# A fused attention and ternary feed-forward kernel: ternary weights from magnitude and sign, six heads of the first pair turned by another route, and one step of the tail put elsewhere

## The chip, the cores and the metric

The kernel runs on one core of a Trainium2 chip. A core has five engines with a queue of instructions each: TensorE (PE in the profile; its weight loads are PEld), VectorE (DVE), ScalarE (ACT), GpSimd (POOL) and SyncE (SP, which only issues transfers). The engines share the on-chip memory SBUF; TensorE writes its results to the accumulators in PSUM. Each engine works through its queue in order and waits at an instruction until what it needs is there. The metric is the device time of one execution in microseconds. Before the change it is 1085.36 us, the median of 3 runs (1084.41 to 1085.46).

## The reference

Sixteen sequences of 256 tokens with 256 features go through an attention layer and a feed-forward layer, each between two layer norms and added to its input. Cut to what is computed:

```python
# attention; H = 16 heads of D = 128
q = (x @ Wq.T).reshape(b, n, H, D)
kp, vp = split(x @ Wkv.T)                 # one K and one V for all heads
kh, vh = cumsum((x @ Wkvh.T) * exp(cumsum(log_sigmoid(x @ Wg.T))))   # one number per head and token
k, v = kp * kh, vp * vh                   # so the heads differ by a factor per token
p = softmax(causal(rope(q) @ rope(k).T / sqrt(D)))
attention = (p @ v).reshape(b, n, H * D) @ Wout.T

# feed-forward; hidden size 1024
def ternary_quant(w):                     # groups of 64 weights
    w = w.astype(bfloat16)
    scale = max(mean(abs(w_group)), 1e-8)
    q = clip(round(w / scale), -1, 1)     # -1, 0 or 1
    return w + (q * scale - w)
gate, up = split(x @ ternary_quant(w_gate_up).T)
ffn = rms_norm(silu(gate) * up) @ ternary_quant(w_proj).T

x = x + layernorm(attention(layernorm(x)))
x = x + layernorm(ffn(layernorm(x)))
```

## The kernel before

**Tiling.** Two sequences make a pair, so that a pair has 512 columns (T); there are 8 pairs. Pair and head together number 128 *slots*: slot g deals with pair g // 16 and head g % 16, in a software pipeline. `slot(g)` writes out, for all engines, the scores of head g; the division of the probabilities of head g-1 by their row sums and the turning of that 256x256 matrix (the product with the values needs it transposed); the keys of head g+2 (`keys`, L659, on POOL); the query product of head g+1 (g+2 in the first four slots) and its rotation on DVE (L347, L355, L358); and the outputs of an earlier head, which ACT copies to `oT` (L802). The projection of the heads and the feed-forward of the pair finished before run in the same slots as guests.

**Order.** Nothing is scheduled at run time. The order in which the program writes instructions is the order of each engine's queue. Guests are put into named places of a slot (first, scored, turned, emptied, projection, last) with `put(slot, place, step, key)`, and the table `MOVED` (L13 to L38) shifts a step by its key through these places, by so many places earlier or later. After slot 127 the function `end()` writes the tail out by hand: the feed-forward of the last three sequences, named there c, a and b (b is sequence 15).

**Two ways to turn probabilities.** `Head.on_pe` (L601) chooses. True: `turn_on_pe` has TensorE transpose three 128x128 blocks for each sequence of the pair (L757) into PSUM, and ACT copies them to SBUF in two pieces each (L762), multiplying by the head's value factors on the way; the outputs then use the shared values, and are written in the same slot. False: ACT's division (L723) writes its four results into the tile `even` in an order by 32 columns; `turn` has DVE transpose all 32x32 blocks at once (L730), SP writes the tile to a buffer in the chip's memory (`moved`, L737) and reads it back with the blocks in their places in four transfers (`pT`, L743); `scale_values` has POOL make this head's values (`vph`, L771), and the outputs (L787, L794) are written one slot later. Before the change, `on_pe` is true for the 16 heads of pair 0 and for the last two heads of the last pair; the other 110 heads go by DVE.

**Ternary weights.** The feed-forward weights come as 12 blocks of 128x512 (8 of gate and up, `gu`, and 4 of the projection, `p`), each handled by one object of `Ternary`. Block i starts around slot 1 + 3i/2, so that the 12 blocks stretch over slots 0 to about 21, shifted by `MOVED` (keys T0 to T11). The steps of one block:

- `load` (L194): POOL issues the transfer of the block in float32.
- `magnitudes` (L198): ACT takes the absolute value, as bfloat16 (`ab`).
- `narrow` (L208): POOL casts the weights to bfloat16 (`wb`). Two tiles t0 and t1, of two halves each, hold `wb`, `sc`, `up` and `dn`.
- `sums` (L212): TensorE multiplies `ab` by a block matrix of ones, so that each row gets the sum of its group (`wsum`).
- `compare`: DVE makes the scale `sc` (L216), then `up` = (edge · sc < wb) at L219 and `dn` = (-edge · sc > wb) at L222. `up - dn` is the ternary digit.
- `combine` (L228 to L231): POOL takes up - dn, times sc, minus wb, plus wb.
- `write` (L234): ACT copies the result to the weights that TensorE reads.

**Tail.** The end of `end()` turns the last projections into output rows. For sequence b: `project(2)`, then `project_rows(0)` and `project_rows(1)`, each the last matmuls (L981) of 128 rows into one half of the accumulator `ffn`; `end_moments(t)` (L1064, L1065: moments of one half, DVE), `end_factors`, `end_centred` and `end_rows(t)` (the row update on DVE and the store by SP). They are interleaved with those of sequence a.

Of the kernel before, what the change touches and what calls it, by code (L numbers as in the profile page):

```python
# [37 lines left out]
AF = mybir.ActivationFunctionType  # L38
ALU = mybir.AluOpType
# [4 lines left out]
H, D = 16, 128  # L44
# [17 lines left out]
TERNARY_EDGE = 257.0 / 512.0  # L62
# [3 lines left out]
def sandwich_kernel(  # L66
# [13 lines left out]
    nc = tc.nc  # L80
# [15 lines left out]
    pairs = B // BP  # L96
# [28 lines left out]
    def load_wq(first, end):  # L125
        cols = slice(first * D, end * D)
        nc.sync.dma_start(
            out=wq_sb[:, :, cols], in_=wq[:, cols].rearrange("(c p) f -> p c f", p=P)
        )
# [55 lines left out]
    def hidden_tile(shape, dtype, name):  # L185
        return p1.tile(shape, dtype, tag="h", name=name, bufs=5)

    class Ternary:
        def __init__(self, dst, src, name):
            self.dst, self.src, self.name = dst, src, name  # L190
# [7 lines left out]
            nc.scalar.activation(self.ab, self.w, AF.Abs)  # L198

        def narrow(self):  # L200
            self.wb, self.sc, self.up, self.dn = (
                pair[:, k, :]
                for pair in [
                    hidden_tile([P, 2, T], BF16, f"t{j}_{self.name}") for j in range(2)
                ]
                for k in range(2)
            )
            nc.gpsimd.tensor_copy(self.wb, self.w)  # L208

        def sums(self):  # L210
            self.total = mm_tile([P, T], f"wsum_{self.name}")
            nc.tensor.matmul(self.total, blocks, self.ab, start=True, stop=True)  # L212

        def compare(self):
            sc, wb = self.sc, self.wb
            nc.vector.tensor_scalar(  # L216
                sc, self.total, 1.0 / GROUP, 1e-8, ALU.mult, ALU.max
            )
            nc.vector.scalar_tensor_tensor(  # L219
                self.up, sc, TERNARY_EDGE, wb, ALU.mult, ALU.is_lt  # L220
            )
            nc.vector.scalar_tensor_tensor(  # L222
                self.dn, sc, -TERNARY_EDGE, wb, ALU.mult, ALU.is_gt
            )

        def combine(self):
            up = self.up
            nc.gpsimd.tensor_sub(up, up, self.dn)  # L228
            nc.gpsimd.tensor_mul(up, up, self.sc)
            nc.gpsimd.tensor_sub(up, up, self.wb)  # L230
            nc.gpsimd.tensor_add(up, up, self.wb)  # L231
# [140 lines left out]
    class Pair:  # L372
# [195 lines left out]
        def plan(self):  # L568

            end = self.bp * H  # L570
            pre = "P." if self.bp > 1 else "Q."
            s = end - H - (2 if self.bp > 1 else -1)
            for b in range(BP):
                put(s + b, "scored", lambda b=b: self.moments(b), key=f"{pre}mom{b}")
                put(s + b, "emptied", lambda b=b: self.normalise(b), key=f"{pre}nor{b}")
                put(s + 2 + b, "turned", lambda b=b: self.transpose(b), key=f"{pre}tp{b}")
                put(s + 2 + b, "emptied", lambda b=b: self.keep(b), key=f"{pre}keep{b}")
            put(s + 4, "last", self.factors, key=f"{pre}hg")
            put(s + 5, "first", self.gates, key=f"{pre}gate")
            put(s + 5, "scored", self.raw_factors, key=f"{pre}raw")  # L580
            put(s + 5, "last", self.keys, key=f"{pre}kp")
            put(s + 7, "scored", lambda: self.rope.sine(0), lambda: self.rope.sine(1), key=f"{pre}ksin")
            put(s + 7, "emptied", self.keys_done, key=f"{pre}kr")
            chain = end - (7 if self.bp > 1 else 8)
            put(chain - 2, "emptied", self.sigmoids, key=f"{pre}sig")
            put(chain - 1, "emptied", self.decays, key=f"{pre}dec")
            put(chain, "scored", self.decayed, key=f"{pre}decd")
            put(chain + 1, "scored", self.sums, key=f"{pre}sum")
            put(chain + 2, "first", self.rows_out, key=f"{pre}rows")
            put(chain + 3, "last", self.value_factors, key=f"{pre}vh")  # L590
            put(chain + 4, "first", self.value_factors_done, key=f"{pre}vhd")
            put(end - 1, "last", self.values, key=f"{pre}val")
            put(end, "first", self.values_done)


    class Head:
        def __init__(self, pair, h):
            self.pair, self.h = pair, h
            self.tag = f"{pair.bp}_{h}"

            self.on_pe = pair.bp == 0 or pair.bp == pairs - 1 and h >= H - 2  # L601

        def fetch_on_pe(self):

# [668 lines left out]
    def end():  # L1273

        c, a, b = afters[B - 3 :]
# [133 lines left out]
        a.end_centred(1)  # L1409
        b.project(2)  # L1410
        b.project_rows(0)
        b.end_moments(0)
        a.end_rows(0)
        b.end_factors(0)
        b.project_rows(1)
        a.end_rows(1)
        b.end_moments(1)
        b.end_factors(1)
# [49 lines left out]
    for g in range(total):  # L1468
        slot(g)
    end()  # L1470


# [37 lines left out]
```

## Time and profile before

| what | value |
|---|---|
| median of 3 runs | 1085.36 us |
| profiled execution | 1085.46 us, its span 1083.7 us |
| PE busy | 1067.4 us (98%) |
| DVE busy | 846.4 us (78%) |
| ACT busy | 734.5 us (68%) |
| POOL busy | 670.7 us (62%) |
| mean bandwidth of the transfers | 127 GB/s |
| comparisons L219 and L222 | 12 each |
| groups of three transposes L757 | 32 in pair 0, 4 in the last pair |
| start of slots 11, 14, 17, 18, 21 on PE | 97.34, 119.10, 140.87, 147.09, 169.92 us |

The page describes one execution. "Busy" is the time in which an engine has an instruction running; the matmul times are modelled, and as matmuls overlap, a row's mean is longer than the pace at which they follow each other. Where a row ends with "[1.10 <-PE ffn L981]", the engine stood idle for 1.10 us before it, and PE's instruction of line 981 is what it waited for. In a row of the costliest groups, the first two numbers are the busy sum in us and the mean of one in ns; behind the next bar stand the idle time before such instructions and what ended most of it. In a table of stretches the columns are the stretch, its length, and the busy time of PE, PEld, DVE, ACT and POOL with the number of instructions in brackets, then the mean granted clock of TensorE, the busy share of the transfer engines and their GB/s. A slot's start is taken as the start of its first score product (L671) on PE.

### The profile page before, as it was taken

To read this page: it belongs to the slowest core of one execution; us is meant where nothing else is said; L and a number is where in the kernel's file an instruction comes from. 1 tells how busy PE (TensorE), PEld (TensorE's weight loads), DVE (VectorE), ACT (ScalarE), POOL (GpSimd) and SP (SyncE) were. 2 spreads that over 40 slices of the span, in tenths; PEclk is the share of its full clock that TensorE was granted. 3 is DMA by queue.
4 is the path that set the end of the run, shared out by engine and by line. 5 is a ranking of instruction groups with operands and counts; after the bars stand their busy time and mean duration, and the time that the engine had idled before them with its cause. 6 is when DMAs were issued, how large, how long until landed. Compare 5 with 4: busy or idle time off the path is not lost.

```text
span 1083.7 us, 18439 instructions
## 1 busy us (share of the span) xinstructions
PE 1067.4 (98%) x5704; PEld 854.3 (79%) x5704; DVE 846.4 (78%) x2306; ACT 734.5 (68%) x2151; POOL 670.7 (62%) x705
## 2 busy tenths in 40 slices
PE   8999999999999999999999999999999999999997
PEld 5767767788788877888778887888868888788897
DVE  6888989877887779868798777978789677876565
ACT  4877866666776658576586766766577675867663
POOL 5966897338555676457665576655756546736443
PEclk9999999999999999999999999999999999999998
DMA  6312134454444444444354444445444444443200
GB/s 229 112 53 77 62 112 153 148 169 122 141 141 134 146 132 141 146 133 143 126 148 134 144 145 132 146 122 160 131 130 151 125 135 136 152 138 111 69 11 30
DMA packets 108625, 137.34 MB, mean 127 GB/s; under 512 B 12208, under 2 KB 76208, under 8 KB 108528
## 3 DMA queue, kind: packets, MB, share of 16 engines
q1 hardware_dynamic: 105696, 129.02, 38.7%
q0 software_dynamic: 2000, 6.56, 1.8%
q8 instruction: 46, 0.75, 0.3%
q10 hardware_dynamic: 832, 0.59, 0.2%
q14 instruction: 51, 0.42, 0.1%
HBM read 88.41 MB, written 47.71 MB: 126 GB/s over the span
## 4 chain that ended last, share of the span: by engine, by line
PE 89%; DVE 8%; ACT 1%; issue 1%; POOL 0%; DMA 0%; DVEq 0%; POOLq 0%; ACTq 0%
PE qps L325 19%; PE att L831 18%; PE sps L671 14%; PE ops L787 9%; PE ffn L981 6%; PE ups L885 5%; PE gps L885 5%; PE ops L794 5%; DVE turned_q L347 2%; PE hg L325 1%; PE vps L325 1%; DVE prob L684 1%; PE kp L325 1%; DVE qps L355 1%; DVE qT L358 1%; PE tps L757 1%
## 5 line engine op out<-in xcount | busy, mean ns | idle before, releaser
L684 DVE CUSTOM_DVE_ANT_0 prob<-sps,mask 128x128 f32<-128x128 f32 (+1 forms) x512 | 160.9, 354 | 122.4 <-PE sps L671 119.3
L802 ACT COPY oT<-ops 128x512 f32<-128x512 f32 x128 | 75.0, 586 | 257.5 <-PE ops L794 257.4
L325 PE MATMUL qps<-xnT,wq_sb 128*128 128x512 f32 x512 | 241.8, 594 | 0.8
L694 ACT ACTIVATE prob<-prob,low 128x128 f32<-128x128 f32 (+1 forms) x512 | 225.7, 444 | 18.3 <-DVE low L684 18.1
L831 PE MATMUL att<-wout_sb,oT 128*128 128x256 f32 x1024 | 237.7, 379 | 0.0
L831 PEld LDWEIGHTS att<-wout_sb,oT 128*128 128x128 f32 x1024 | 188.5, 190 | 30.2 <-issue 8.6
L771 POOL TENSOR_TENSOR vph<-vp,vh 128x512 f32<-128x512 f32 x110 | 115.9, 1054 | 132.1 <-PE ops L794 132.0
L671 PE MATMUL sps<-kT,qT 128*128 128x128 f32 (+1 forms) x1024 | 192.1, 331 | 4.1 <-DVE qT L358 2.2
L347 DVE TENSOR_TENSOR turned_q<-qps,sin_sb 64x512 f32<-64x512 f32 (+1 forms) x258 | 176.0, 682 | 15.0 <-PE qps L325 9.5
L659 POOL TENSOR_TENSOR kT<-kh,kr 128x512 f32<-128x512 f32 x128 | 164.6, 1286 | 7.9 <-PE sps L671 7.2
L723 ACT ACTIVATE even<-prob,total 128x128 f32<-128x128 f32 (+1 forms) x440 | 163.9, 447 | 1.1 <-DVE total L705 1.1
L671 PEld LDWEIGHTS sps<-kT,qT 128*128 128x128 f32 x1024 | 145.0, 191 | 21.4 <-issue 7.3
L325 PEld LDWEIGHTS qps<-xnT,wq_sb 128*128 128x128 f32 x512 | 95.2, 190 | 71.7 <-issue 61.6
L787 PE MATMUL ops<-pT,vph 128*128 128x256 f32 x440 | 131.3, 380 | 0.9 <-POOL lo L931 0.7
L931 POOL TENSOR_TENSOR lo<-h,hi 128x512 fp32r<-128x512 f32 x54 | 69.1, 1279 | 97.3 <-ACT hi L929 93.1
L730 DVE STREAM_TRANSPOSE sq<-even 128x768 f32<-128x768 f32 x110 | 107.5, 977 | 13.9 <-ACT even L723 10.9
L694 ACT ACTIVATION_READ_ACCUMULATOR prob<-prob,low 128x1 f32 x512 | 96.9, 189 | 0.0
L355 DVE TENSOR_TENSOR qps<-qps,cos_sb 128x512 f32<-128x512 f32 (+1 forms) x129 | 89.5, 694 | 4.6
L794 PEld LDWEIGHTS ops<-pT,vph 128*128 128x128 f32 x440 | 83.5, 190 | 11.4
L358 DVE TENSOR_TENSOR qT<-qps,turned_q 128x512 f32<-128x512 f32 (+1 forms) x129 | 88.5, 686 | 4.5
L949 POOL TENSOR_TENSOR squares<-squares,sq 128x512 f32<-128x512 f32 x39 | 49.8, 1277 | 63.3 <-ACT sq L948 63.3
L794 PE MATMUL ops<-pT,vph 128*128 128x128 f32 x440 | 84.5, 274 | 0.0
(167 smaller groups left out, 1924.8 us busy)
## 6 DMA issues: line engine op xcount, KB each, us to landing
moved<-sq SPq DMA_DIRECT2D x110, 384.0 KB, 2.3
pT<-moved SPq DMA_DIRECT2D x440, 96.0 KB, 2.2
kh<-rows SPq DMA_DIRECT2D x126, 256.0 KB, 3.4
xt<-in_x_dram SPq DMA_DIRECT2D x15, 256.0 KB, 3.0
out_dram<-y POOLq DMA_DIRECT2D x13, 256.0 KB, 3.3
wout_sb<-in_wout_dram SPq DMA_DIRECT2D x2, 1024.0 KB, 9.6
w_gu<-in_wgu_dram POOLq DMA_DIRECT2D x8, 256.0 KB, 3.4
wq_sb<-in_wq_dram SPq DMA_DIRECT2D x1, 1536.0 KB, 9.5
```

Source lines behind the costliest of these rows:

```text
L325: nc.tensor.matmul(ps, lhs[:, c, :], rhs[:, c, :], start=(c == 0), stop=(c == EC - 1))
L347: self.engine.tensor_mul(by_sequence(self.turned[a : a + HALF, :]), by_sequence(self.src[b : b + HALF, :]), over_sequences(sin_sb[b : b + ...
L659: nc.gpsimd.tensor_mul(self.kT, self.kh, self.pair.kr)
L671: nc.tensor.matmul(sps[:, cols], self.qT[:, n0 + i * P : n0 + (i + 1) * P], self.kT[:, n0 : n0 + (i + 1) * P], start=True, stop=True,)
L684: nc.vector.tensor_tensor_reduce(out=prob[:, cols], in0=sps[:, cols], in1=mask[:, P - i * P :], scale=-SCALE, scalar=F32_MAX, op0=ALU.add, ...
L694: nc.scalar.activation(prob[:, cols], prob[:, cols], AF.Exp, bias=low[:, i : i + 1], scale=-1.0, accum_out=self.total[:, b * 2 + i : b * 2 ...
L723: nc.scalar.activation(dst, src, AF.Copy, scale=self.total[:, 2 * b + i : 2 * b + i + 1])
L771: nc.gpsimd.tensor_mul(self.vp, self.pair.vp, self.pair.vh[:, :, self.h : self.h + 1].to_broadcast([P, NT, D]),)
L787: nc.tensor.matmul(ops[:, n0 : n0 + N], self.vp[:, b * (N // P), :], early, start=True, stop=False,)
L794: nc.tensor.matmul(ops[:, n0 + P : n0 + N], self.vp[:, b * (N // P) + 1, :], late, start=False, stop=True,)
L831: nc.tensor.matmul(self.acc[:, t, :], oT[:, n0 + t * P : n0 + (t + 1) * P], wout_sb[:, h, :], start=(h == 0 and t == 0), stop=(h == H - 1) ...
L885: nc.tensor.matmul(ps[:, k, :], wgu_sb[:, c, (f0 + k) * P : (f0 + k + 1) * P], part[:, c, :], start=(i == 0), stop=(i == len(steps) - 1),)
```

## The change

Three things change.

1. *Ternary.* `narrow` gets a second step: ACT writes the sign of the weights (-1, 0 or 1) where `dn` was. `compare` makes one comparison instead of two, of the scale with the magnitude `ab`. `combine` begins with `up * sign` instead of `up - dn`. Everything else of a block, and the places of its steps, stay.
2. *Heads.* `on_pe` is true only for heads 0 to 9 of pair 0. Heads 10 to 15 of pair 0, which are turned in slots 11 to 16, take the way over DVE, SP's transfers and POOL, and their outputs are written one slot later: slot 11 then has no outputs, and slots 12 to 17 have those of heads 10 to 15. (In the kernel before, slot 17 is the one without: head 0 of pair 1 is written in slot 18.)
3. *Tail.* `b.project_rows(1)` stands directly behind `b.project_rows(0)`, ahead of the moments of the first half, instead of behind `b.end_factors(0)`.

```diff
 def narrow(self):
-    self.wb, self.sc, self.up, self.dn = (
+    self.wb, self.sc, self.up, self.sign = (
...
     nc.gpsimd.tensor_copy(self.wb, self.w)
+    nc.scalar.activation(self.sign, self.w, AF.Sign)
...
 def compare(self):
-    sc, wb = self.sc, self.wb
+    sc = self.sc
     nc.vector.tensor_scalar(
         sc, self.total, 1.0 / GROUP, 1e-8, ALU.mult, ALU.max
     )
     nc.vector.scalar_tensor_tensor(
-        self.up, sc, TERNARY_EDGE, wb, ALU.mult, ALU.is_lt
-    )
-    nc.vector.scalar_tensor_tensor(
-        self.dn, sc, -TERNARY_EDGE, wb, ALU.mult, ALU.is_gt
+        self.up, sc, TERNARY_EDGE, self.ab, ALU.mult, ALU.is_lt
     )
...
 def combine(self):
     up = self.up
-    nc.gpsimd.tensor_sub(up, up, self.dn)
+    nc.gpsimd.tensor_mul(up, up, self.sign)
     nc.gpsimd.tensor_mul(up, up, self.sc)
     nc.gpsimd.tensor_sub(up, up, self.wb)
     nc.gpsimd.tensor_add(up, up, self.wb)
...
 class Head:
-    self.on_pe = pair.bp == 0 or pair.bp == pairs - 1 and h >= H - 2
+    self.on_pe = pair.bp == 0 and h < 10 or pair.bp == pairs - 1 and h >= H - 2
...
 def end():
     b.project_rows(0)
+    b.project_rows(1)
     b.end_moments(0)
     a.end_rows(0)
     b.end_factors(0)
-    b.project_rows(1)
     a.end_rows(1)
     b.end_moments(1)
```

The places in which `slot(g)` writes what belongs to the two ways:

```python
if before and not before.on_pe:
    before.turn()                  # DVE transpose, SP's five transfers
if before and before.on_pe:
    before.turn_on_pe(0)           # PE, ACT
if g + 2 < total:
    all_heads[g + 2].keys()        # POOL
all_heads[g + ahead].queries()     # PE
if before and not before.on_pe:
    before.scale_values()          # POOL
if before and before.on_pe:
    before.turn_on_pe(1)
...
if before and before.on_pe:
    before.outputs()
if 2 <= g < total + 2 and not all_heads[g - 2].on_pe:
    all_heads[g - 2].outputs()
```

## The prediction

> **What bounds the kernel now.** I read the page's head and chain first, then the stretch in which the edited heads and weight blocks lie, then the last 10 us.
>
> ```profile
> span 1083.7 us, 18439 instructions
> PE 1067.4 (98%) x5704; PEld 854.3 (79%) x5704; DVE 846.4 (78%) x2306; ACT 734.5 (68%) x2151; POOL 670.7 (62%) x705
> PE 89%; DVE 8%; ACT 1%; issue 1%; POOL 0%; DMA 0%; DVEq 0%; POOLq 0%; ACTq 0%
> 97.34:169.92 72.58, 69.91 (x331) 50.41 (x330) 63.83 (x169) 55.38 (x176) 63.22 (x63) 1.00 0.30 97
> ```
>
> TensorE is the bound, and the clock is full. The last line (busy PE, PEld, DVE, ACT, POOL from the start of slot 11 to that of slot 21) shows something the page's averages hide: here POOL is busy for 63.2 of 72.6 us, DVE for 63.8, PE for 69.9. Work moved from PE to DVE and POOL goes to engines with 9 us of slack each.
>
> **Part 1: six heads turned elsewhere.** The page gives a transpose 273 ns, but matmuls are pipelined; what counts is when the next group starts:
>
> ```profile
> 120.50 0.49 PE L757 MATMUL tps<-ident,prob 128*128 128x128 f32 x3
> 120.83 1.88 PE L325 MATMUL qps<-xnT,wq_sb 128*128 128x512 f32 x4
> L730 DVE STREAM_TRANSPOSE sq<-even 128x768 f32<-128x768 f32 x110 | 107.5, 977 | 13.9 <-ACT even L723 10.9
> L771 POOL TENSOR_TENSOR vph<-vp,vh 128x512 f32<-128x512 f32 x110 | 115.9, 1054 | 132.1 <-PE ops L794 132.0
> ```
>
> Three transposes hold PE for 120.83-120.50 = 0.33 us, so 6 heads x 2 groups x 0.33 = **3.9 us** leave PE (by the busy row it would be 9.8). ACT loses four PSUM copies per head (L762, 1.21 us from the start of the first to that of what follows, 7.3 in all); its four divisions stay at 446 ns, writing another layout. Added: 6 x 0.98 = 5.9 us on DVE, 6 x 1.01 (start to start) = 6.1 us on POOL, and per head five DMAs on SP: one of 384 KB, four of 96 KB. These sit behind the key fetch of the same slot and ahead of the next; that fetch feeds a product two slots later. From the end of a DVE transpose (144.06) to the last of its four issues (148.33) plus 2.2 us to land is 6.4 us; outputs now stand one slot later, about 7.7 us after the transpose, so some 1.3 us remain. The loads of x for pair 2 queue behind these too; the second would go out near 124.7 instead of 114.8 and is wanted at 128.
>
> Could DVE take it? In slots 11 to 16 it loses four of part 2's comparisons (0.68, 2.09, 2.07, 0.68 = 5.5 us) and gains 5.9. Per slot it then has scores 1.41, transpose 0.95, rotation of the next queries 1.42 + 0.73 + 0.61, reciprocal 0.1: 5.2 us; a weight block adds 0.66 + 0.69, the moments of pair 2 0.95. PE has scores 1.4, queries 1.72, projection 1.73, outputs 1.3: 6.15, in slot 11 no outputs, which come back in slot 17. The rotation ends after PE in slots 11 (103.4 against 102.5) to 16, so DVE releases the next scores. Adding these rows with small gaps, slots 12 to 17 start at 103.4, 110.2, 117.0, 124.1, 131.8, 138.4; before at 104.7, 111.6, 119.1, 126.2, 134.0, 140.9. The lead is **2.5 us** at slot 17.
>
> **Part 2: magnitude and sign.** Twelve L222 comparisons leave DVE, 13.7 us busy; twelve Sign calls join ACT, not in the trace. Lower bound 0 (hidden), upper the sibling Abs on the same tile, 632 ns; I take its pace, 0.53. The multiplication by the sign costs POOL what the subtraction did (1.16).
>
> ```profile
> 112.89 2.09 DVE L222 SCALAR_TENSOR_TENSOR t_gu<-t_gu 128x512 bf16<-128x512 bf16 x1
> 113.14 1.28 POOL L659 TENSOR_TENSOR kT<-kh,kr 128x512 f32<-128x512 f32 x1
> L694 ACT ACT_TABLE_LOAD x13 | 16.7, 1283 | 0.2
> ```
>
> Two rules bear on this. The Trainium skill, *ScalarE: Activation LUTs*, "Table sets: the hidden batching unit", says that functions come in sets that must be loaded, and names relu, copy, identity and abs as those that every set has. Sign is not named there. If it were missing from Exp's set, every block would cost two loads, 24 x 1.283 = 30.8 us of ACT; the trace shows Abs between Exps without a load and cannot show Sign. I take none, and keep 30.8 as a remote end. *SBUF — State Buffer*, "Who interferes with whom", says a DVE instruction with two SBUF inputs and a GpSimd one exclude each other, the later waiting out the earlier. The rows differ with overlap: L222 took 2.09 us beside the key product, 0.68 elsewhere. By the rows part 2 frees 13.7 us; by the rule it frees 12 x 0.68 = 8.2 of work, and the six added POOL products bring back new collisions for the twelve comparisons that stay (up to 2.3 each, if one meets a key product and a value product). DVE has 2.5 us to spare before slot 17, so I count nothing for this, and 1 us in the range.
>
> In slots 2 to 4 ACT holds PE (chain from 29.92 to 33.65). Two Signs come before the divisions of head 2: 2 x 0.53, less 0.3 of wait that is there, puts PE 0.75 us back; it regains it at 47.95, where it waited 0.7 us behind a comparison. Slots 5 to 10 have 0.7 us of PE idle in all. Net 0 (-0.5 to +0.3).
>
> **Where the lead of 2.5 us goes.** Five lines around slot 17, whose last PE item is the sum over block 10 (wsum_p):
>
> ```profile
> 103.68 0.78 POOL L194 DMA_DIRECT2D w_p<-in_wproj_dram  x1 [3.37 <-ACT ab_gu L198]
> 143.18 1.16 POOL L231 TENSOR_TENSOR t_p<-t_p,t_p 128x512 bf16<-128x512 bf16 x1
> 144.70 1.13 ACT L234 CAST wproj_sb<-t_p 128x512 fp32r<-128x512 bf16 x2
> 145.72 0.63 ACT L198 ACTIVATE ab_p<-w_p 128x512 bf16<-128x512 f32 x1
> 146.41 0.38 PE L212 MATMUL wsum_p<-ab_p,blocks 128*128 128x512 bf16 x1 [0.18 <-ACT ab_p L198]
> ```
>
> POOL ends block 9 at 144.3, ACT copies it, takes block 10's magnitudes, PE sums them and only then starts slot 18. POOL's queue from the load at 103.68 to 144.3 is 40.6 us, of which 3.1 are waits for DVE (1.24 + 0.64 + 0.62 + 0.64): 37.5 of work. After: plus five value products, 5.1, is 42.6, without waits. It starts earlier, since ACT lost a head's copies (1.21) and gained a Sign (0.53): 103.0. So block 9 ends at 145.6; less 0.3 (half of what one POOL pair, 3.09 instead of 2.44, lost to a comparison now gone), 145.3. ACT, free at 142, waits for it, then copy 0.52, Sign 0.54, copy 0.52, Abs 0.63: PE's sum at 147.55 and slot 18 at 147.75 against 147.09. PE has stood idle since about 144.9 (138.4 + 6.15 + 0.44 for pair 2's transposes). Queued behind that wait are slot 18's scores; next late is its query product, which takes the bank of block 10's sum. DVE must read that first, and waits for POOL's cast of block 10 (145.3 + load 0.8 + keys 1.24 + values 1.01 + cast 0.6 = 148.95), so queries start at 149.6 against 148.64: **1.0 us late**. Afterwards PE is full to slot 20, and POOL has caught up by the pair's means at 165. The 3.9 us are spent waiting.
>
> **Part 3: b.project_rows(1) earlier.**
>
> ```profile
> 1076.42 0.43 DVE L1064 BATCH_NORM_STATS2 st_c<-ffn 128x6 f32<-128x256 f32 x1 [1.10 <-PE ffn L981]
> 1076.91 0.58 PE L981 MATMUL ffn<-wproj_sb,hi 128*128 128x256 f32 x1 [0.53 <-DVE st_c L1064]
> 1078.16 0.43 DVE L1064 BATCH_NORM_STATS2 st_c<-ffn 128x6 f32<-128x256 f32 x1 [0.25 <-PE ffn L981]
> ```
>
> Now PE's second half waits for DVE's moments of the first: the accumulator is tracked as one tile. Turned round, the first moments wait for both halves. PE ends at 1075.97 + 4 x 0.213 (its pace there) + 0.41 = 1077.23; moments at 1077.27; then in DVE's order 0.46 + 0.10 + two row updates with a small step between, 0.39 + 0.07 + 0.39: second moments at 1078.7 instead of 1078.16. **+0.55 us**, and nothing lies behind it but the last rows and their store.
>
> **Sum**, against the profiled execution, 1085.46 (span 1083.7 and 1.8 around it; 0.1 above the median): -2.5 lead, +3.5 wait, +0.55 end: 1087.0, +0.14% on the median 1085.36. A measurement of this kernel tells about 0.2%, 2.2 us, from no change.
>
> **Rivals.** (a) PE keeps its lead: POOL's block 9 done by 142, or the sum not reached by then. For: PE is 89% of the chain. Against: POOL's 42.6 us. 1085.46-2.5+0.55 = 1083.5; all 3.9 kept, 1082.1. (b) Slower: block 11's weights. Its Sign stands in ACT ahead of the head's outputs, block 11's magnitudes, slot 17's division and slot 18's exponentials. The load goes out at 145.3 and landed 3.0 us after its issue ended before (1.27 us of ACT wait). That gives 149.1, with DVE reaching qT of slot 19 at 156.3 against PE's 158. Beyond 1.7 us more each us is one lost: at 6 us, 1088.5; with collisions, 1090. (c) The transposed blocks land late: one transfer took 4.3 us (151.70 to 155.96) instead of 2.4; at 0.6 us of stall over six slots, 3.6, less the 2.5 lead, 1088.1. (d) Sign reloads tables: at least half of 30.8 shows, 1102. (e) Early gain larger, POOL never late: 1084.5.
>
> **Chances.** Main case 0.52 (own range 1085.4 to 1088.2), a 0.13, b 0.16, c 0.12, d 0.02, e 0.05. Main: a quarter lies above 1087.53, 0.13 slower; of b 0.15, of c 0.10, and d 0.02: slower 0.40. Faster (under 1083.2): two thirds of a and a little of e, 0.10. Same 0.50. The range 1083.3 to 1089.6 leaves out the fuller end of a, the far ends of b and c, and d.
>
> **What would show it.** Right: one comparison row in the place of two, 1.5 us or more of PE idle before slot 17's wsum_p, with ACT's copy waiting for block 9's last POOL step, PE ahead by 1 to 3 us at slot 16, the last moments one after the other. Wrong: table loads above 28; outputs of heads 10 to 15 waiting on pT; scores of slot 18 earlier than 146.5 or later than 149.

## The result, and the profile after

The changed kernel takes 1090.94 us (median of 4 runs, 1089.55 to 1092.15) against 1085.15 us for the kernel before in the same comparison. The ratio is 1.005, with a 95% interval of 1.0038 to 1.0062: it is slower by about 5.8 us. The prediction was 1087.0 us with a range of 1083.3 to 1089.6; the time lies above it. The profiled execution took 1091.06 us, its span 1089.1 us, 5.4 us more than before. (From `combine` on, line numbers of the kernel after are lower by 2: its key product is L657, its value product L769.)

From the page of the kernel after: its head, busy times and the shares of its chain.

```profile
span 1089.1 us, 18413 instructions
PE 1065.6 (98%) x5668; PEld 853.0 (78%) x5668; DVE 846.8 (78%) x2300; ACT 733.5 (67%) x2139; POOL 673.8 (62%) x711
PE 87%; DVE 6%; POOL 2%; ACT 2%; issue 1%; DMA 1%; DVEq 0%; SPq 0%; POOLq 0%
```

TensorE has less to do and the kernel is longer. In the chain PE and DVE have each lost 2% of the span, to POOL, ACT and the transfers. Where the time went is read from the starts of the slots on PE (first score product, after minus before):

| slot | 10 | 11 | 12 | 13 | 14 | 17 | 18 | 21 | 22 | 127 | end of span |
|---|---|---|---|---|---|---|---|---|---|---|---|
| us | -0.3 | +0.5 | -0.4 | +1.0 | +2.0 | +1.9 | +3.7 | +3.6 | +5.3 | +5.2 | +5.4 |

So time is lost in four places: slot 10, slots 12 and 13, the way from slot 17 to 18, and slot 21. Slot 11 wins 0.9 us back, because it has no outputs now; they follow in slot 17 and are 1.3 us of what is lost there. From slot 22 on the two kernels run in step, and the tail adds 0.2.

**Slot 10.** The first two rows are of the kernel before, the others of the kernel after (start in us, duration; in brackets what the engine waited for):

```profile
89.18 1.35 DVE L484 TENSOR_TENSOR_SCAN summed<-ones,raw 64x256 f32<-64x256 f32 x1
90.54 1.29 POOL L659 TENSOR_TENSOR kT<-kh,kr 128x512 f32<-128x512 f32 x1
...
88.85 2.28 DVE L482 TENSOR_TENSOR_SCAN summed<-ones,raw 64x256 f32<-64x256 f32 x1
89.30 1.28 POOL L657 TENSOR_TENSOR kT<-kh,kr 128x512 f32<-128x512 f32 x1
91.69 0.84 PE L755 MATMUL tps<-ident,prob 128*128 128x128 f32 x3 [0.76 <-ACT prob L721]
```

With one comparison less, POOL is through with a weight block 1.2 us sooner, and its key product, which came after DVE's running sum (the scan) before, now lies across it. The sum takes 2.28 us instead of 1.35; ACT's division waits 1.21 us for the reciprocal behind it, and PE 0.76 us for ACT. That the key product is the cause was not tested by a run of its own, but the rows agree: the sum takes 2.07 to 2.28 us in every run with one comparison, and 0.77 to 1.38 in every run with two.

**Slots 12 and 13.** DVE's comparisons of two blocks in the kernel before (the fourth of them stands in the prediction), then the timeline of the kernel after, rows of POOL, DVE and PE in order of time:

```profile
105.31 1.56 DVE L219 SCALAR_TENSOR_TENSOR t_gu<-t_gu 128x512 bf16<-128x512 bf16 x1
106.80 0.68 DVE L222 SCALAR_TENSOR_TENSOR t_gu<-t_gu 128x512 bf16<-128x512 bf16 x1
112.23 0.73 DVE L219 SCALAR_TENSOR_TENSOR t_gu<-t_gu 128x512 bf16<-128x512 bf16 x1
...
104.86 1.28 POOL L657 TENSOR_TENSOR kT<-kh,kr 128x512 f32<-128x512 f32 x1
104.92 2.77 DVE L220 SCALAR_TENSOR_TENSOR t_gu<-t_gu,ab_gu 128x512 bf16<-128x512 bf16 x1
106.08 1.06 POOL L769 TENSOR_TENSOR vph<-vp,vh 128x512 f32<-128x512 f32 x1
...
112.62 1.58 PE L669 MATMUL sps<-kT,qT 128*128 128x128 f32 x8 [1.98 <-DVE qT L356]
113.27 2.91 DVE L220 SCALAR_TENSOR_TENSOR t_gu<-t_gu,ab_gu 128x512 bf16<-128x512 bf16 x1
113.34 1.28 POOL L657 TENSOR_TENSOR kT<-kh,kr 128x512 f32<-128x512 f32 x1
114.56 1.05 POOL L769 TENSOR_TENSOR vph<-vp,vh 128x512 f32<-128x512 f32 x1
118.46 0.67 PE L785 MATMUL ops<-pT,vph 128*128 128x256 f32 x2 [0.82 <-DMA pT<-moved]
121.11 1.58 PE L669 MATMUL sps<-kT,qT 128*128 128x128 f32 x8 [1.10 <-DVE qT L356]
```

The one comparison that is left (L220; L219 before) takes 2.77 and 2.91 us. It ends about half a microsecond after POOL's value product in both cases. Before, with no value product in these slots, the comparisons L219 and L222 of the same two blocks took 1.56 + 0.68 and 0.73 + 2.09. The stretches from slot 12 to 13 and from 13 to 14 show what this makes of DVE (length of the stretch, then busy PE, PEld, DVE, ACT, POOL):

```profile
104.14:112.62 8.48, 6.51 (x28) 4.65 (x28) 8.23 (x18) 3.91 (x13) 7.61 (x9) 1.00 0.55 156
112.62:121.11 8.49, 6.57 (x28) 4.69 (x28) 8.34 (x17) 4.45 (x14) 7.59 (x9) 1.00 0.64 186
```

DVE (third busy number) is taken for 8.2 to 8.3 of 8.5 us, the waits inside its comparisons included: it is the bound here, and PE (first) idles for 2 us of each slot.

**Slot 18.** The rows of the kernel after that answer to those shown around slot 17 before:

```profile
147.13 1.16 POOL L229 TENSOR_TENSOR t_p<-t_p,t_p 128x512 bf16<-128x512 bf16 x1
148.32 0.62 ACT L232 CAST wproj_sb<-t_p 128x512 fp32r<-128x512 bf16 x1 [2.29 <-POOL t_p L229]
148.84 0.62 ACT L209 ACTIVATE t_p<-w_p 128x512 bf16<-128x512 f32 x1
149.37 0.60 ACT L232 CAST wproj_sb<-t_p 128x512 fp32r<-128x512 bf16 x1
149.88 0.62 ACT L198 ACTIVATE ab_p<-w_p 128x512 bf16<-128x512 f32 x1
150.56 0.38 PE L213 MATMUL wsum_p<-ab_p,blocks 128*128 128x512 bf16 x1 [1.06 <-ACT ab_p L198]
```

This is the chain that the prediction described: POOL's last step of block 9, ACT's copy of it, Sign, a copy and magnitudes, then PE's sum and slot 18. PE waits 1.06 us.

**Slot 21.** The start of slot 21 before, and two stretches of 3.41 us around it in the kernel after, where it starts at 173.52; the third number from the end is the granted clock:

```profile
169.92 1.58 PE L671 MATMUL sps<-kT,qT 128*128 128x128 f32 x8 [1.52 <-DVE qT L358]
...
170.29:173.70 3.41, 1.46 (x9) 1.17 (x8) 3.27 (x7) 2.93 (x10) 3.33 (x5) 1.00 0.41 147
173.70:177.11 3.41, 3.41 (x10) 2.53 (x10) 2.67 (x11) 2.98 (x9) 3.41 (x4) 0.50 0.48 128
```

PE was busy for only 1.46 of 3.41 us, and then had half the clock for exactly 3.41 us: 1.7 us lost. The kernel before waits 1.52 us here and has no half clock.

**Costs named in the prediction that did not come.** Of the groups of ACT, in the kernel after:

```profile
L692 ACT ACT_TABLE_LOAD x13 | 16.7, 1283 | 0.2
L209 ACT ACTIVATE t_gu<-w_gu 128x512 bf16<-128x512 f32 x8 | 5.1, 633 | 0.0
```

The table loads are 28 as before, and a Sign costs 0.63 us, as the magnitudes do.

### The profile page after: what moved, and what is told of

The parts are those of the page before. It is cut to its first block, busy times and chain, and to the rows that moved or that the text cites. A ratio compares the mean times of both kernels' runs of the same rounds, so it can differ in the third digit from the quotient of the medians.

```text
span 1089.1 us, 18413 instructions
## 1 busy us (share of the span) xinstructions
PE 1065.6 (98%) x5668; PEld 853.0 (78%) x5668; DVE 846.8 (78%) x2300; ACT 733.5 (67%) x2139; POOL 673.8 (62%) x711
## 4 chain that ended last, share of the span: by engine, by line
PE 87%; DVE 6%; POOL 2%; ACT 2%; issue 1%; DMA 1%; DVEq 0%; SPq 0%; POOLq 0%
PE qps L323 18%; PE att L829 18%; PE sps L669 13%; PE ops L785 9%; PE ffn L979 6%; PE ups L883 5%; PE gps L883 5%; PE ops L792 5%; DVE prob L682 1%; PE hg L323 1%; PE vps L323 1%; PE kp L323 1%; DVE turned_q L345 1%; DVE sq L728 1%; PE tps L755 1%
## 5 line engine op out<-in xcount | busy, mean ns | idle before, releaser
L769 POOL TENSOR_TENSOR vph<-vp,vh 128x512 f32<-128x512 f32 x116 | 122.4, 1055 | 134.2 <-PE ops L792 134.1
L721 ACT ACTIVATE even<-prob,total 128x128 f32<-128x128 f32 x464 | 172.8, 447 | 4.1 <-DVE total L703 3.9
L657 POOL TENSOR_TENSOR kT<-kh,kr 128x512 f32<-128x512 f32 x128 | 163.4, 1277 | 7.9 <-PE sps L669 7.2
L785 PE MATMUL ops<-pT,vph 128*128 128x256 f32 x464 | 138.6, 380 | 1.5 <-DMA pT<-moved 0.8
L728 DVE STREAM_TRANSPOSE sq<-even 128x768 f32<-128x768 f32 x116 | 113.2, 976 | 13.5 <-ACT even L721 10.5
L792 PEld LDWEIGHTS ops<-pT,vph 128*128 128x128 f32 x464 | 88.1, 190 | 12.0
L792 PE MATMUL ops<-pT,vph 128*128 128x128 f32 x464 | 89.1, 274 | 0.0
```

Of the source, the lines that this page charges most:

```text
L657: nc.gpsimd.tensor_mul(self.kT, self.kh, self.pair.kr)
L721: nc.scalar.activation(dst, src, AF.Copy, scale=self.total[:, 2 * b + i : 2 * b + i + 1])
L728: nc.vector.transpose(turned.rearrange("p k u q -> p (k u q)"), self.even.rearrange("p k u q -> p (k u q)"),)
L769: nc.gpsimd.tensor_mul(self.vp, self.pair.vp, self.pair.vh[:, :, self.h : self.h + 1].to_broadcast([P, NT, D]),)
L785: nc.tensor.matmul(ops[:, n0 : n0 + N], self.vp[:, b * (N // P), :], early, start=True, stop=False,)
L792: nc.tensor.matmul(ops[:, n0 + P : n0 + N], self.vp[:, b * (N // P) + 1, :], late, start=False, stop=True,)
```

## The experiments

Each time is a median, set beside runs of the kernel before in the same comparison (1085.36 for the first four experiments, 1085.34 for the next four, 1085.76 for the last four).

### One part at a time

**Part 1 alone** (`e1_heads_only`):

```diff
-self.on_pe = pair.bp == 0 or pair.bp == pairs - 1 and h >= H - 2
+self.on_pe = pair.bp == 0 and h < 10 or pair.bp == pairs - 1 and h >= H - 2
```

> The kernel before with part 1 alone (six heads turned by DVE; two comparisons per weight block, tail as before). Theory A, formed from the profile after (a comparison with two inputs in SBUF waits for the end of POOL's back-to-back key and value product, so that DVE becomes the bound in slots 12 to 14): one of the two comparisons of each block still meets the pair, 2.8 us, and the other adds 0.69, so slot 17 starts 3 to 4 us later than before (144 to 145 against 140.87) and the kernel takes 1090 to 1092. The theory on record (DVE has slack, POOL's queue holds up slot 18 by about 1 us): slot 17 at most 1 us late, 1085.5 to 1087.

Measured: 1094.14 us, ratio 1.0076 (1.0064 to 1.0088). The loss was larger than either theory said: slot 17 starts 7.8 us late. Three comparisons here took 2.30, 2.85 and 3.16 us, each over a key and a value product of POOL. TensorE waited for DVE three times for 2.2 to 3.8 us, and half clocks followed.

**Part 2 alone** (`e2_sign_only`): the kernel after with `on_pe` and the tail as before.

> Part 2 alone (sign on ACT, one comparison on DVE, all heads of pair 0 turned by TensorE, tail as before). Theory A: without the new value products a comparison meets at most the key product of 1.28 us, the twelve comparisons sum to 14 to 16 us (23.8 for the 24 before), DVE is nowhere the bound, and the time stays: 1084.5 to 1085.5. If instead the Sign calls on ACT are what costs, the loss shows here: 1086 to 1088.

Measured: 1086.31 us, ratio 1.0005 (0.9997 to 1.0013): no difference that can be told, though the median lies where a cost of the Sign calls was expected. Its profile shows the loss in slot 10 (0.8 us) and is 0.5 us late at slot 127; by the rows that is the longer running sum, not the Sign calls. The twelve comparisons sum to 14.2 us, as expected of a comparison that meets the key product alone. Against part 1 alone, though, the other two parts bring some 3 us back (ratio 1.0076 to 1.005). The dropped comparison helps where DVE is the bound.

**Part 3 alone** (`e3_tail_only`):

```diff
 b.project_rows(0)
+b.project_rows(1)
 b.end_moments(0)
 a.end_rows(0)
 b.end_factors(0)
-b.project_rows(1)
```

> Part 3 alone (the second half of the last projection ahead of the first half's moments). The step on record: the last moments 0.55 us later, 1085.7. Rival, from the profile after, where only 0.2 us of that reached the end of the span: 1085.2 to 1085.4. Either way not more than 0.6 us of the whole loss.

Measured: 1085.58 us, ratio 0.9997 (0.9989 to 1.0005). A cost of 0.55 us lies at the edge of that interval; it can't be told from none. The profiles of this run and of part 2 alone, which has the old tail, can be compared more closely, as the half clock begins 55.3 us after the start of slot 127 in both: the last row update starts 66.21 us after it here and 65.74 there, so that part 3 costs 0.47 us. So most of the loss is part 1's.

### What makes the comparisons long

`e4_one_sbuf_input`, on the kernel after:

```diff
 nc.vector.scalar_tensor_tensor(
-    self.up, sc, TERNARY_EDGE, self.ab, ALU.mult, ALU.is_lt
+    self.up, self.total, TERNARY_EDGE / GROUP, self.ab, ALU.mult, ALU.is_lt
 )
```

> The changed kernel, but the comparison reads the group sum from PSUM (edge/64 times the sum, compared with the magnitude) instead of the scale in SBUF, so that it has one input in SBUF; the threshold is then not rounded to bfloat16 first. POOL's and ACT's work stay the same. Theory A: no comparison waits for POOL, all twelve take 0.6 to 0.75 us (8.5 in all instead of 18.4), slots 13 and 14 lose their idle time, slot 17 starts at 138 to 140 instead of 142.7, and only the wait before slot 18 remains: 1086 to 1088. Rival B (the six transposes themselves are too much for DVE, the comparisons are long only because they wait anyway): slot 17 stays after 142 and the time near 1090.9.

Measured: 1088.36 us, ratio 1.0028 (1.002 to 1.0037). The timeline of this run, rows of POOL, DVE and SP:

```profile
104.44 0.68 DVE L220 SCALAR_TENSOR_TENSOR t_gu<-wsum_gu,ab_gu 128x512 bf16<-128x512 f32 x1
104.59 1.28 POOL L657 TENSOR_TENSOR kT<-kh,kr 128x512 f32<-128x512 f32 x1
105.82 1.05 POOL L769 TENSOR_TENSOR vph<-vp,vh 128x512 f32<-128x512 f32 x1
...
126.87 0.43 SPq L107 DMA_DIRECT2D xt<-in_x_dram  x1
131.06 0.75 DVE L270 BATCH_NORM_STATS2 st_a<-xt 128x6 f32<-128x256 f32 x2 [3.17 <-DMA xt<-in_x_dram]
```

The comparison beside the same key product takes 0.68 us instead of 2.77, and so do all twelve (8.1 us in all, 18.4 in the kernel after). POOL's two products take what they took. That shows the mechanism: DVE's second input from SBUF and POOL's work exclude each other. It is the rule that the Trainium skill states in *SBUF — State Buffer*, "Who interferes with whom"; the same section says that an instruction with one SBUF input does not contend outside the modes that use both ports, and here the trace agrees. With it gone, slots 13, 14 and 15 start 1.3, 1.6 and 1.7 us *earlier* than before: most of the lead that the prediction worked out for them (1.4, 2.1, 2.1) is there, although the running sum of slot 10 still takes 2.09 us.

Then it is lost to something that the slower kernel had hidden. DVE waits 3.17 us for the load of pair 2's x, which SP issued at 126.87 behind the turned blocks. In the kernel after, the same load went out at 128.49 and DVE came to it at 131.82 without waiting. PE's gap before slot 16 (3.58 us) and the one before slot 21 were each followed by a half clock, so that slot 17 starts at 142.96, where 138 to 140 was expected.

`e5_x_earlier` is that kernel with the load moved:

```diff
-put(pair.bp * H - 19 + b, "last", lambda q=q: load_x(q, nc.sync), key=f"L{b}")
+put(pair.bp * H - 19 + b - (2 if pair.bp == 2 else 0), "last", ...)
```

> The kernel with one SBUF input in the comparison, and in it the two loads of pair 2's x issued two slots earlier, ahead of the first transfers of the turned blocks. There VectorE stood still for 3.17 us until the second load had landed. If SyncE's queue is what made it late, the idle time before slot 16 (3.58 us) goes, slots 16 and 17 keep the lead of 1.7 to 2.5 us (slot 17 at 138.4 to 139.3), and the half clock that followed at 136 goes with it. What is left is the wait ahead of slot 18 for ScalarE and GpSimd (slot 18 at 147.5 to 148.5), and perhaps a half clock at slot 21: 1084.5 to 1087. If the load is late for another reason (the memory, the buffer), slot 16 stays near 135.

Measured: 1089.49 us, ratio 1.0034 (1.0022 to 1.0046). The expected gain did not come. The wait for x is gone, but others stand in its place. The timeline of PE and ACT:

```profile
117.36 0.67 PE L785 MATMUL ops<-pT,vph 128*128 128x256 f32 x2 [2.13 <-DMA pT<-moved]
...
148.91 0.38 PE L213 MATMUL wsum_p<-ab_p,blocks 128*128 128x512 bf16 x1 [1.71 <-ACT ab_p L198]
150.64 0.63 ACT L209 ACTIVATE t_p<-w_p 128x512 bf16<-128x512 f32 x1 [1.78 <-DMA w_p<-in_wproj_dram]
151.64 0.59 ACT L390 COPY xnT<-tp_a 128x512 f32<-128x512 f32 x1
152.28 1.98 PE L323 MATMUL qps<-xnT,wq_sb 128*128 128x512 f32 x4 [1.69 <-ACT xnT L390]
```

Slot 13's outputs waited 2.13 us for the turned block, because SP's write of it took 4.6 us to land instead of the usual 2.3, and a half clock followed. It was issued at 107.09, 2.2 us after a key fetch of 256 KB, and overlapped with it; in the kernel after it was issued at 109.72, behind the landing of the fetch, and took 3.7 us. Ahead of slot 18 PE waited 1.71 us for block 10's magnitudes. And then it waited 1.69 us more: Sign of block 11 stood in ACT's queue until its load had landed, and the copy of pair 2's transposed x, whose accumulator the next query product takes over, stood behind it.

### GpSimd's queue ahead of slot 18

`e6_write_later`, on the kernel of `e5_x_earlier`; the entry moves ACT's copy of block 9 behind the magnitudes of block 10:

```diff
-"T9.ma": -4, "T9.na": -1,
+"T9.ma": -4, "T9.na": -1, "T9.wr": 2,
```

> The same with the loads earlier, and ScalarE's copy of weight block 9 moved behind the magnitudes of block 10, so that TensorE's group sum of block 10 no longer waits for GpSimd's block 9. The step on record (POOL's block 9 holds up ACT, ACT the sum, the sum slot 18) says that slot 18 comes 1 to 2 us earlier than without this move, at 145.5 to 146.5, and that the time falls by as much: 1083 to 1085.5. If the sum is held by something else, such as the landing of block 10 or the cast, the time stays.

Measured: 1091.27 us, ratio 1.0057 (1.0044 to 1.007). The move itself did what was expected, and the time grew. The timeline of ACT and PE:

```profile
147.71 0.38 PE L213 MATMUL wsum_p<-ab_p,blocks 128*128 128x512 bf16 x1
149.96 0.63 ACT L209 ACTIVATE t_p<-w_p 128x512 bf16<-128x512 f32 x1 [3.44 <-DMA w_p<-in_wproj_dram]
152.12 2.58 PE L323 MATMUL qps<-xnT,wq_sb 128*128 128x512 f32 x4 [2.73 <-ACT xnT L390]
```

The sum no longer waits, and comes 1.2 us earlier (147.71 against 148.91). But ACT arrives at block 11's Sign sooner and stands there for 3.44 us; PE then waits 2.73 us for ACT, and a half clock follows. POOL issues that load only after its block 9 (at 145.69 here). So both ways out of slot 17 end at POOL's queue, and to reorder ACT only changes which one shows.

`e7_values_on_act` takes load off POOL. On the kernel after:

```diff
-nc.gpsimd.tensor_mul(self.vp, self.pair.vp, ...)
+if self.pair.bp == 0:
+    for j in range(NT):
+        nc.scalar.activation(self.vp[:, j, :], self.pair.vp[:, j, :], AF.Copy,
+                             scale=self.pair.vh[:, j, self.h : self.h + 1])
+else:
+    nc.gpsimd.tensor_mul(self.vp, self.pair.vp, ...)
```

> The changed kernel, with the values of the six moved heads scaled by ScalarE (four copies with a scale of 128x128) instead of by GpSimd (one product). Theory A: a comparison then meets the key product alone, so the two long ones of slots 12 and 13 fall from 2.77 and 2.91 to 1.6 to 2.1, the sum of the twelve from 18.4 to about 15, slot 17 comes 1.5 to 2 us earlier, and as GpSimd has 6.3 us less to do before block 9, the wait ahead of slot 18 shrinks by a further 1 us or more: 1086 to 1088. Rival B (the transposes alone fill DVE): slot 17 stays at 142 to 143. A cost of its own: ScalarE has 1.2 to 1.6 us more in each of six slots.

Measured: 1089.96 us, ratio 1.0041 (1.0025 to 1.0056). In the profile the comparisons sum to 14.3 us, but the two long ones still take 2.46 and 1.92 (1.6 to 2.1 was expected), and slot 13 starts 1.2 us late. POOL ends block 9 at 145.0 instead of 148.3, and slot 18 starts without the wait for ACT. Slot 17 is 1.2 us and slot 18 2.4 us earlier than in the kernel after. ACT's own cost shows as 1.33 us of wait for magnitudes in slot 11. The median lies above the expected 1086 to 1088; the runs spread from 1085.5 to 1093.1, so it tells little.

### The half clock

`e8_gap_filled`, on the kernel after: in slot 20 the outputs are computed twice.

```diff
-for b in range(BP):
+for b in range(BP) if not fill else [0, 1, 0, 1]:
...
+if g == 20:
+    all_heads[g - 2].outputs(fill=True)
```

> The changed kernel with the outputs of slot 20 computed twice over (1.3 us of TensorE work for nothing, in the 1.95 us in which TensorE stands idle before slot 21). Theory C (idle time of more than about half of a stretch of 3.4 us makes the chip grant half the clock for the next 3.4 us): with the gap filled slot 21 starts at the same time, the half clock there does not come, slot 22 follows 7.9 us after slot 21 instead of 9.6, and the kernel gets about 1.7 us faster, 1089 to 1089.7, by doing more. Rival: the half clock is not set off by the gap, and the time stays at 1090.9 or grows by up to 1.3.

Measured: 1091.05 us, ratio 1.0055 (1.0042 to 1.0068). In its profile the clock stays full up to the tail, and slot 22 follows slot 21 after 7.88 us instead of 9.56. Two stretches of it, from slot 20 to 21 and the next 3.41 us:

```profile
166.69:173.69 7.00, 5.98 (x29) 4.39 (x29) 6.86 (x24) 5.67 (x17) 5.66 (x8) 1.00 0.53 153
173.69:177.10 3.41, 3.41 (x16) 2.32 (x15) 2.49 (x11) 3.21 (x10) 3.41 (x4) 1.00 0.63 186
```

So the gap set off the half clock there. The median did not fall, however; this profile, the longest of its runs, has a late turned block in slot 31 (0.97 us) and a longer half clock in the tail. How often the half clock at slot 21 comes in the kernel after stays open: one profile shows it once.

### Fewer heads, and what is left when the walls are taken away

`e12_three_heads`: the kernel after with `h < 13` in place of `h < 10`.

> The changed kernel with only heads 13 to 15 of pair 0 turned by VectorE (10 to 12 by TensorE as before). TensorE saves 2.0 us instead of 3.9. The two long comparisons (2.77 and 2.91 us, in slots 11 and 12) then meet no value product. Theory A: they fall to about 2.0 and 0.8, VectorE is not the bound there, slot 14 starts within 0.5 us of before; slot 18 still waits for GpSimd's block 9, three value products late instead of five: 1 us late. 1086 to 1088. If instead the loss goes with the number of transposes, half of it stays: 1088.

Measured: 1089.51 us, ratio 1.0029 (1.0019 to 1.0039). In its profile the comparisons of the first two blocks in question took 2.05 and 0.80, as expected, and slots 14 and 15 start 0.1 us earlier than before. PE then waits 1.67 us for DVE ahead of slot 15, a half clock follows (slot 16 is 1.2 us late), and slot 18 loses 0.8 us. At slot 127 this profile is 1.3 us behind the kernel before, at the end of the span 0.4; but it is the shortest of the eight runs (1085.99 us), and the median lies above what either theory said. So the profile bears out the comparisons' part, and what the longer runs lose besides stays open.

The last three change several things at once. `e9_two_plain` is the kernel before, its two comparisons with the accumulator as first input (the threshold is then not rounded to bfloat16 first, here and in the other kernels with this edit):

```diff
-self.up, sc, TERNARY_EDGE, wb, ALU.mult, ALU.is_lt
+self.up, self.total, TERNARY_EDGE / GROUP, wb, ALU.mult, ALU.is_lt
...
-self.dn, sc, -TERNARY_EDGE, wb, ALU.mult, ALU.is_gt
+self.dn, self.total, -TERNARY_EDGE / GROUP, wb, ALU.mult, ALU.is_gt
```

> The kernel before, with both comparisons reading the group sum from PSUM instead of the scale in SBUF (threshold not rounded first); nothing else. Theory A: the 24 comparisons fall from 23.8 us to 16 to 16.5 us, all at 0.67 to 0.69. VectorE is waited for only here and there in this kernel (0.35 us before slot 9, 0.31 before slot 18), so the time falls by no more than 0.3 to 1 us: 1084.3 to 1085.1.

Measured: 1084.18 us, ratio 0.9987 (0.9978 to 0.9995), faster than both kernels. The 24 comparisons take 16.3 us.

`e10_balanced` adds to it the six heads, their values on ACT and pair 2's x five slots earlier:

> The six heads turned by VectorE as in part 1, with the three costs that the runs so far showed taken out of their way: both comparisons with one SBUF input (no Sign on ScalarE), the values of the six heads scaled by ScalarE, pair 2's x loaded five slots earlier; tail as before. GpSimd and ScalarE then have as much to do as in the kernel before, VectorE about 2 us more over six slots. If exclusion, GpSimd's queue and the late load were all that ate the 3.9 us, slot 17 starts at 138 to 139.5, slot 18 at 145 to 146.5 and the kernel takes 1082 to 1084. If the turned blocks then arrive late (0.8 to 2.1 us at slot 13 in the runs with an early TensorE), 1084 to 1086.

Measured: 1084.36 us, ratio 0.9987 (0.998 to 0.9994). The stretch from slot 11 to 21 in its profile (columns as in the stretches above):

```profile
96.62:167.72 71.10, 66.11 (x296) 47.23 (x294) 63.47 (x175) 55.09 (x176) 60.06 (x62) 1.00 0.51 158
```

The waits of PE in this stretch that are over half a microsecond, from its timeline:

```profile
102.45 0.90 PE L212 MATMUL wsum_gu<-ab_gu,blocks 128*128 128x512 bf16 x2 [0.80 <-ACT ab_gu L198]
115.37 0.67 PE L796 MATMUL ops<-pT,vph 128*128 128x256 f32 x2 [0.52 <-DMA pT<-moved]
122.42 0.38 PE L212 MATMUL wsum_p<-ab_p,blocks 128*128 128x512 bf16 x1 [0.75 <-ACT ab_p L198]
167.72 1.58 PE L671 MATMUL sps<-kT,qT 128*128 128x128 f32 x8 [1.96 <-DVE qT L358]
```

With POOL and ACT loaded as before and no exclusion, slot 17 starts 2.7 us earlier than in the kernel before and slot 21 2.2 us earlier: the 71.1 us of this stretch are 72.6 before. But `e9_two_plain`, without the six heads, is 1.3 us early at both slots already. Of the lead, the heads with the two other moves make 1.4 us at slot 17 and 0.9 at slot 21, though PE has 3.6 us less to do in this stretch (66.1 against 69.7), and the medians are the same.

`e11_balanced_sign` is all three parts with the comparison from the accumulator, the values on ACT and x five slots earlier:

> All three parts of the change, with the comparison reading PSUM, the six heads' values scaled by ScalarE and pair 2's x loaded five slots earlier. Against the run with values on ScalarE alone VectorE's waits before slots 13, 14 and 16 (1.77, 0.77, 0.93) should go, and ScalarE's before the group sum of slot 11 (1.33, it has a Sign more in the queue) stay: 1085 to 1087. If it is not slower than the version without Sign, ScalarE's queue does not matter.

Measured: 1087.99 us, ratio 1.0021 (1.0014 to 1.0029), above the expected 1085 to 1087 and slower by 3.6 us than the version with two comparisons, no Sign and the old tail. Its profile shows the running sum of slot 10 at 2.09 us (0.77 there), waits of 1.33 and 1.26 us for magnitudes behind the Signs in slots 11 and 14, 1.49 us before slot 18's queries behind block 11's Sign, and the half clock at slot 21. So Sign is not free once ACT has the heads' values too; what each of these costs of the 3.6 us was not separated.

## Why the prediction was wrong

**The step that failed** stands in part 1: "In slots 11 to 16 it loses four of part 2's comparisons (0.68, 2.09, 2.07, 0.68 = 5.5 us) and gains 5.9." A row's 2.09 us was taken to be the cost of that instruction. It was a wait for POOL, and when the instruction goes, the wait passes to the one that stays. The four blocks' comparisons went from 9.19 us to 8.25 (2.77, 2.91, 1.10, 1.47): a relief of 0.94 us, not 5.5. Slot 17 shows it: 1.9 us late where 2.5 us early was forecast. Of these 4.4 us, 0.9 are missing at slot 12 already (0.4 us early, 1.3 forecast), after the running sum of slot 10, another DVE instruction with two inputs in SBUF, which the prediction leaves out; by slot 14 it is 4.1 (2.0 late, 2.1 early forecast). Part 2 names the rule, the bound ("up to 2.3 each, if one meets a key product and a value product") and then says "DVE has 2.5 us to spare before slot 17, so I count nothing for this". That spare time had been worked out with the collisions left out. The bound was good: 2.77 and 2.91 are 0.68 and 2.1 to 2.2.

**Where the lead goes, slot 18.** The mechanism was right, with the engine, the block and the order of ACT's queue; its time was 3.0 us off, 148.3 instead of 145.3 for POOL's end of block 9, since the queue, taken to run without waits, had waited for DVE (0.64 + 0.64 + 1.31 us). PE's idle time there was 1.06 us, as PE was late itself. That slot 18 then loses 1.8 us against slot 17 comes mostly from the outputs (1.3 us) that slot 17 has now and slot 11 has not. The second wait, of slot 18's query product for DVE's scale behind POOL's cast, did not come; where TensorE was early enough (`e5_x_earlier`, `e6_write_later`, `e11_balanced_sign`) that product waited 1.5 to 2.7 us for ACT, behind block 11's Sign. That is the mechanism of rival (b), at another place in the queue.

**The rivals.** (c), late transfers, had a price of 0.6 us per slot; the kernel after shows one wait of 0.82 us, and 2.13 in the run with an early TensorE. The margin of 1.3 us worked out for these transfers was too thin there, where one write alone took 4.6 us to land. The load of pair 2's x was found ("near 124.7 ... wanted at 128") and given no price; it was worth 3.2 us as soon as DVE was on time. (a) and (e) were out, because DVE never let the lead arise. (d) did not happen: no table load more.

**Parts that held.** TensorE's saving as work: 3.6 us of the forecast 3.9 (`e10_balanced` against `e9_two_plain`). Part 2 up to the start of slot 10: -0.3 us, forecast -0.5 to +0.3; then slot 10 itself lost 0.8. Part 3: 0.47 us in the two runs with the same clock in the tail, forecast 0.55. In the kernel after, from the start of the last projections the last moments stand at 6.06 us instead of 5.51, but there the clock of the two tails differs; at the end of the span 0.2 is left, as the last row update was followed by 2.8 us of store instead of 3.1. The rows of the kernel after that answer to those shown of the tail:

```profile
1082.46 0.43 DVE L1062 BATCH_NORM_STATS2 st_c<-ffn 128x6 f32<-128x256 f32 x1 [1.45 <-PE ffn L979]
1083.88 0.42 DVE L1062 BATCH_NORM_STATS2 st_c<-ffn 128x6 f32<-128x256 f32 x1
```

The second moments follow the first without a wait for PE, behind the row updates of sequence a.

**What was not thought of** is the clock: the prediction says that it is full and leaves it there, and takes 0.213 us as the pace of the last projection without noticing that the clock is halved in the tail (at full clock the same products follow each other every 0.12 us). At slot 21 a wait that grew from 1.52 to 1.95 us cost 1.7 us beyond itself.

Two slips of the working do not bear on this: slot 12 of the kernel before starts at 104.53, not 104.7, and the terms of rival (c) add up to 1087.1, or to 1088.1 only with slot 18's 1.0 us on top.

The sum of the profiled execution: +1.9 (up to slot 17, forecast -2.5), +1.8 (slot 18), +1.5 (half clock at slot 21, 1.7, less 0.2 regained) and +0.2 (tail) make the 5.4 us of the span.

## What to carry to other kernels

A long row of an instruction that another engine can shut out is partly a wait: before counting it as saved, ask what it was waiting for and which instruction meets that now; if it can read one input from PSUM, the wait is gone for a change of one operand. Work moved to an engine with slack on average must be laid into its queue slot by slot, together with the loads that share the queue of its transfers. When the bound engine gets faster, the next walls stand close behind each other (here DVE, pair 2's load, turned blocks, POOL's block 9, ACT's queue), so that taking away one alone moved the time little.

## What the runs showed of the hardware that was not expected

- Half clock after half-idle stretches. The clock records lie on a grid of 3.41 us. In the slots of the fourteen profiles, TensorE's rows leave 1.92 us or more of such a stretch idle in ten cases (1.92 to 2.45), and after each at least the next 3.41 us had half the clock. Of the stretches with 1.77 to 1.86 idle one had it too, the others went without, as did those below. For these the line thus lies somewhat above half. The Trainium skill, *TensorE: Matmul & The Clock Gate*, "What's actually happening", gives a free-running window of that length and says that the clock falls after an idle window; here a window idle by 56% was enough. A wait of 1.95 us therefore costs up to 3.65, an estimate from these rows, depending on where it falls in the grid: waits of 1.94 to 1.96 us before slot 21 in `e5_x_earlier`, `e6_write_later` and `e10_balanced` lay across two stretches and cost no clock. (The shares are worked out from PE's rows, whose ends are modelled.)
- Busy rows do not always keep the clock. Two stretches in the tail of the kernel before:

```profile
1070.34:1073.75 3.41, 3.41 (x31) 3.41 (x32) 0.92 (x3) 0.08 (x1) 0.00 (x0) 1.00 0.02 5
1073.75:1077.16 3.41, 2.88 (x14) 2.59 (x14) 2.08 (x11) 0.84 (x2) 1.09 (x2) 0.50 0.00 0
```

PE is busy throughout the first, and the second has half the clock. In 13 of the 14 profiles the first half clock of the tail comes so, after a stretch in which 2.2 to 2.7 us are products of a single column (L960); in `e12_three_heads` these lay across two stretches, 2.0 and 1.7 us, and none followed. What the chip counts as activity is left open. The length of the tail goes with the place of the half clock: the old tail took 67.6 us from the start of slot 127 in the kernel before, where the half clock began after 57.7 us, and 69.3 us in `e2_sign_only`, where it began after 55.3.
- A comparison of 128x512 in bfloat16 takes 0.68 us with one input in PSUM, in all its places beside POOL's work (12 or 24 in each of six runs), and up to 3.4 us with both in SBUF, by what POOL happens to run.
- A write of 384 KB, with a median of 2.3 us to landing, took 4.6 us when issued 2.2 us after a fetch of 256 KB. That the fetch slowed it was not tested by itself; the kernel before has single writes of up to 4.5 us too.
